# Two projections behind the shared expert's last steps, and list pairs taken five in four experts

## The chip, the core and the metric

The kernel runs on one core of a Trainium2 chip. A core has engines with queues of their own, each in order: TensorE (PE in the profile: matrix products; PEld is its loading of weights), VectorE (DVE), ScalarE (ACT), GpSimd (POOL) and SyncE (SP, which here only issues DMAs). They meet through semaphores. The metric is the time of the device in microseconds (us), from launch to end; lower is better.

## What is computed

The input x is (2, 1024, 256). It is normalized over its last axis (mean and variance, eps 1e-5) to xn. The result is x + attention(xn) + ffn(xn).

The attention reads xn as tokens of 16 numbers on a 64 x 64 grid. One product makes q, k and v. Two branches of 8 channels each attend inside windows of 8 tokens, one along rows, one along columns, with softmax(q k / sqrt(8)) v, and add a 3 x 3 depthwise convolution of v (its window is one token wide, so only three taps of each filter count). A projection, a layernorm with weights and a residual of the tokens follow, and a transpose of tokens and channels.

The ffn is a mixture of 16 experts for 2048 rows of 256, with hidden width 176, and a shared expert of width 352:

```
out[row] = sum over the row's 6 experts e of  weight[row, e] * (silu(x Wg[e]) * (x Wu[e])) Wd[e]
         + (silu(x Sg) * (x Su)) Sd
```

The six experts are chosen by a sigmoid gate with a bias: the two best of four groups of experts, then the six best of what is left. Everything is float32.

## The kernel before

**Stages.** First (to about 60 us) the rows are loaded, normalized and turned (`xnT`), the gate is computed, and each row gets a key by its choice of experts. A sort by that key puts the 2048 rows into 16 tiles of 128, so that rows of a tile share most of their experts. For each tile the six most frequent experts are computed for all its rows, with weight 0 where a row hasn't chosen one: 96 experts in all (kind "six"). What is left over (rows that chose an expert outside their tile's six) is gathered into lists of 128 rows, 14 of them worked off in the main loop (kind "extra") and any rest in a loop at the end.

**The shared expert** is a generator (`shared_steps`, L266) whose steps are taken out by `meanwhile(until)` (L317) between other work: products (L275), the gate on ScalarE (L283) and its product with the other half on VectorE (L284, into `room`), and down products (L290) with the copy and bias on ScalarE (L291). `meanwhile(100)` at L1113 takes all steps that are still left, those of the last block of 512 rows.

**The attention** is a list of steps with costs (`attention`, L657), one head after another: four heads (two halves of the batch, two halves of the columns). A head gathers rows (L670), makes eight projections (`project`, L673: one product on TensorE, L675, and four copies on ScalarE, L677 to L680), four products of q and k (L688) and their sums (L692) on VectorE, the softmax (L698 to L704, with the exponential on ScalarE at L700), four products with v (L709) and sums (L714), the division (L722, `xo`), and transposes on TensorE (L729) with copies on ScalarE (L731, `oT`). The first product of q and k needs projections 0 to 3, the second 4 to 7. After the four heads, `attended` and `normed` project, normalize and add (L781 to L806).

**The main loop** (L1124) runs over 55 units of two experts each (48 "six", 7 "extra"); i = 2u + q counts experts. For each expert, `begun` makes the two up products (L867), the silu on ScalarE (L869, `sg`), and the weighted product on VectorE (L870, `hms`). There are three PSUM buffers for the up products, so an expert can't start before the VectorE step of the third one before it is done. A unit's hidden values are turned one unit later (`hidden`, L881), and the down products follow one unit after that (L893, or L901 for an extra). A finished tile is scattered with accumulation to the output by GpSimd (`to_out`, L1008). Tiles of sorted rows are fetched by GpSimd (`asked`, L827) and turned (`sorted_tile`, L835) ahead of use. `walked` (L1096) takes attention steps in between, as many as the planner's costs allow (`done`, `pace`). Ahead of the loop it is called once with a fixed limit of `FIRST_ROWS - LEAD` (L1111), where the counted time starts at -LEAD and each of the head's first steps (the gathering and the eight projections) counts 0.3.

**The lists** come from a generator, `lists_begun` (L914), of which the loop takes one step per expert from i = 14 on (L1134). After three steps of preparation on VectorE come the pairs of expert and tile that are left over, up to NX = 26, one per step: `pair_listed` reads a column with a register from a table on ScalarE (L967, `spot`, two buffers), and makes a one-hot matrix for it with two GpSimd operations (L969, L970, four buffers in `ysum`). A product on TensorE (L960, `rows_of`) adds it to the lists, two pairs behind. At the end `lists_ended` (L973) turns the sums into row numbers on VectorE (L976, L977), and the extras' rows are gathered by them on GpSimd (`gathered`, L994), one unit ahead of use. The first extra is the 49th expert, i = 48.

**The order.** The source's order is not the queues' order: a scheduler, working from its own estimates while the program is built, places each instruction in its engine's queue. So a small change of the source can move many instructions.

Of the kernel before, what the change touches and what calls it, by code (L numbers as in the profile page):

```python
# [22 lines left out]
P = 128  # L23
# [20 lines left out]
NX = 26  # L44
# [7 lines left out]
def csw_block_moe(ctx: ExitStack, tc: tile.TileContext, x, qkv_w, conv_w0, conv_b0, conv_w1, conv_b1,  # L52
# [20 lines left out]
    nc = tc.nc  # L73
# [78 lines left out]
    for c in range(16):  # L152
        n = sum(P // 2 if k % 2 == 0 else P for k in range(c)) + (((16 - c) * P - 1) / 2 if c % 2 == 0 else 0)
# [380 lines left out]
    for c in range(15, -1, -1):  # L534
        n = 16 - c
# [8 lines left out]
        for k in range(1, n):  # L544
            nc.tensor.matmul(down_[:, c + k : c + k + 1], lhsT=beats[:, k, :], rhs=less[:, c % 2 : c % 2 + 1], start=False,
                             stop=(c == 0 and k == 15))
# [25 lines left out]
    for n in range(2):  # L572
        nc.vector.tensor_tensor(ohp[:, 8 * n : 8 * n + 8], row_h.unsqueeze(1).to_broadcast(wide),
                                place[:, 1, 8 * n : 8 * n + 8].unsqueeze(2).to_broadcast(wide), ALU.is_equal)
        for c in range(8 * n, 8 * n + 8):
# [38 lines left out]
                     start=True, stop=True)  # L614
# [297 lines left out]
    listed = []  # L912

    def lists_begun():  # L914
        flagged = room_[:, 832:960].bitcast(BF16)
        behind = room_[:, 960:1024].bitcast(BF16)
        spot = room_[:, 1024:1280]
        spoti = [t.bitcast(I32) for t in (room_[:, 1280:1536], ysum[:, 7])]
        by_pair = flagged.rearrange("p (e t) -> p e t", t=NTL)
        nc.vector.scalar_tensor_tensor(by_pair, wsrt.rearrange("p t e -> p e t"), 0.0, kept, op0=ALU.is_gt, op1=ALU.mult)  # L920
        nc.vector.tensor_scalar(behind, row_h, part_no, None, op0=ALU.is_gt)
        before = ps_m.tile([P, 2, E * NTL], F32, tag="m", name="before")
        nc.tensor.matmul(before[:, 0], lhsT=behind, rhs=flagged, start=True, stop=True)
        nc.tensor.matmul(before[:, 1], lhsT=ones, rhs=flagged, start=True, stop=True)
        yield
        rows_, some, upto = small.tile([P, E], F32, name="rows_"), small.tile([P, E], I32, name="some"), begin[:, 1]
        nc.vector.tensor_reduce(out=rows_, in_=before[:, 1].rearrange("p (e t) -> p e t", t=NTL), axis=AX.X, op=ALU.add)
        nc.vector.tensor_scalar(some, rows_, P - 1.0, None, op0=ALU.add)
        nc.vector.tensor_scalar(some, some, 7, None, op0=ALU.logical_shift_right)
        nc.vector.tensor_copy(begin[:, 0], some)  # L930
        one_e = one_f.to_broadcast([P, E])
        nc.vector.tensor_tensor_scan(ends, one_e, begin[:, 0], 0.0, op0=ALU.mult, op1=ALU.add)
        nc.vector.tensor_tensor(begin[:, 0], ends, begin[:, 0], ALU.subtract)
        nc.vector.tensor_tensor_scan(upto, one_e, rows_, 0.0, op0=ALU.mult, op1=ALU.add)
        nc.vector.tensor_tensor(upto, upto, rows_, ALU.subtract)
        nc.vector.scalar_tensor_tensor(begin[:, 0], begin[:, 0], float(P), upto, op0=ALU.mult, op1=ALU.subtract)
        nc.vector.tensor_tensor_scan(spot, one_f.to_broadcast([P, E * NTL]), before[:, 1], 0.0, op0=ALU.mult, op1=ALU.add)
        nc.vector.tensor_tensor(spot, spot, before[:, 1], ALU.subtract)
        nc.vector.tensor_tensor(spot, spot, before[:, 0], ALU.add)
        wide = [P, E, NTL]  # L940
        nc.vector.tensor_tensor(spot.rearrange("p (e t) -> p e t", t=NTL), spot.rearrange("p (e t) -> p e t", t=NTL),
                                begin[:, 0].unsqueeze(2).to_broadcast(wide), ALU.add)
        yield
        nc.vector.tensor_copy(spoti[0], spot)
        nc.vector.tensor_scalar(spoti[1], spoti[0], 7, None, op0=ALU.logical_shift_right)
        nc.vector.tensor_scalar(spoti[0], spoti[0], P - 1, None, op0=ALU.bitwise_and)
        nc.gpsimd.memset(at_[:, :, 0:1], 0.0)
        for n in range(2):
            nc.scalar.copy(at_[:, n, 1:], spoti[n])
        nc.vector.tensor_tensor(at_[:, 2, 1:].rearrange("p (e t) -> p e t", t=NTL), by_pair,  # L950
                                of_f.unsqueeze(1).to_broadcast(wide), ALU.mult)
        listed.append(ps_t.tile([P, NX], F32, tag="y1", name="rows_of", padded_shape=[P, TB]))
        yield
        spots = {}
        for n in range(NX + 2):
            if n < NX:
                spots[n] = pair_listed(n)
            if n >= 2:
                spot = spots.pop(n - 2)
                nc.tensor.matmul(listed[0], lhsT=spot[:, 0:P], rhs=spot[:, P:], start=(n == 2), stop=(n == NX + 1))  # L960
            yield
        lists_ended()
        yield

    def pair_listed(n):
        spot = small.tile([P, 3], F32, name="spot", tag="spot")
        nc.scalar.copy(spot, at_[:, :, bass.ds(number(xrow[0:1, 0, n : n + 1], ACT, NTL * E), 1)].rearrange("p a n -> p (a n)"))  # L967
        spots = room_[:, 1024 + 80 * (n % 4) :][:, 0 : (P + NX) // 2].bitcast(F16)
        nc.gpsimd.tensor_scalar(spots[:, 0:P], row_h, spot[:, 0:1], None, op0=ALU.is_equal)  # L969
        nc.gpsimd.tensor_scalar(spots[:, P:], row_h[:, 0:NX], spot[:, 1:2], spot[:, 2:3], op0=ALU.is_equal, op1=ALU.mult)  # L970
        return spots

    def lists_ended():  # L973

        none = room_[:, 1500 : 1500 + NX]
        nc.vector.tensor_scalar(none, listed[0], 0.0, ROWS + 1.0, op0=ALU.is_equal, op1=ALU.mult)  # L976
        nc.vector.scalar_tensor_tensor(lists[:, 0:NX], listed[0], -1.0, none, op0=ALU.add, op1=ALU.add)  # L977

        over = room_[0:1, 0 : NX * E].rearrange("p (n e) -> p n e", e=E)
        of_list = room_[0:1, 500 : 500 + NX]  # L980
        nc.vector.tensor_tensor(over, ends[0:1].unsqueeze(1).to_broadcast([1, NX, E]),
                                number_f[0:1, 0:NX].unsqueeze(2).to_broadcast([1, NX, E]), ALU.is_le)
        nc.vector.tensor_reduce(out=of_list, in_=over, axis=AX.X, op=ALU.add)
        nc.vector.tensor_scalar(xrow[:, 2, 0:NX], of_list, E - 1.0, None, op0=ALU.min)
        nc.vector.tensor_copy(xrow[:, 1, 0:NX], number_f[0:1, 0:NX])

        some = small.tile([1, 2], F32, name="some_")
        nc.vector.scalar_tensor_tensor(some[:, 0:1], pairs_[0:1], NX + 0.5, pairs_[0:1], op0=ALU.is_gt, op1=ALU.mult)
        nc.vector.tensor_tensor(some[:, 0:1], some[:, 0:1], ends[0:1, E - 1 : E], ALU.max)
        nc.vector.tensor_scalar(left, some[:, 0:1], -float(NL), 0.0, op0=ALU.add, op1=ALU.max)  # L990
# [93 lines left out]
    of_tile = (0.75, 0.25)  # L1084
    END = 84
    in_walk = [4 * (16 * 2.3 + 3.3 + 2.5 + 1.5 + 1.4) + 0.6 + 8 * 1.4, 4 * 6.2 + 8 * 3.9]
    FIRST_ROWS, LEAD = 2.5, 12
    done = [float(-LEAD), 0.0]
    whole = [in_walk[n] + NTL * TOPK * of_slot["six"][n] + NL * of_slot["extra"][n] + NTL * of_tile[n] for n in range(2)]
    pace = (whole[0] - LEAD - END * of_slot["six"][0] / of_slot["six"][1]) / (whole[1] - END)  # L1090
# [1 line left out]
    def counted(cost):  # L1092
        for n in range(2):
            done[n] += cost[n]
# [22 lines left out]
    begun_, hT_ = {}, {}  # L1117
    waiting = []
    extras_, lists_ = extras_listed(), lists_begun()

    def fetched(u):
        middle(wts[:, u % 3], *(expert_of(laid_out[u], q, SP) for q in range(2)))

    for u in range(len(laid_out) + 2):  # L1124
        for q in range(2):
            i = 2 * u + q

            while tiles_sorted < NTL and 5 * (tiles_sorted - 2) <= 6 * (i - 2):
                sorted_tile(tiles_sorted)
                counted(of_tile)  # L1130
                tiles_sorted += 1
            while len(asked_for) < min(NTL, tiles_sorted + 3):
                asked()
            if i in (2, 4, 8) or i >= 14:  # L1134
                next(extras_ if i < 14 else lists_, None)
            if u + 1 < len(laid_out) and laid_out[u + 1][0] == "extra":
                n = laid_out[u + 1][1] + q
                ahead[n] = gathered(lists[:, n : n + 1])
            if u < len(laid_out):
                if q == 0:  # L1140
                    fetched(u)
                begun_.setdefault(u, []).append(begun(laid_out[u], q, hms[:, u % 2]))
            if q == 1:
                if 0 <= u - 1 < len(laid_out):
                    hT_[u - 1] = hidden(hms[:, (u - 1) % 2])
                if 0 <= u - 2 < len(laid_out):
                    finished(laid_out[u - 2], hT_.pop(u - 2), wts[:, (u - 2) % 3], begun_.pop(u - 2))
            counted(of_slot[laid_out[min(u, len(laid_out) - 1)][0]])
            walked()
            if done_:  # L1150
                to_out(*done_.pop(0))
            while waiting:
                waiting.pop(0)()
# [73 lines left out]
```

## Time and profile before

| | us |
|---|---|
| median of 3 runs | 449.53 (446.91 to 451.74) |
| the profiled execution | 448.94 |
| its span | 447.2 |
| TensorE busy | 393.4 |
| VectorE busy | 293.0 |
| ScalarE busy | 215.6 |
| GpSimd busy | 187.8 |
| mean granted clock of TensorE | 0.978 |

In the lines that follow, a row of the timeline gives the start from the span's start, the duration, the engine, the line of the kernel, the operation, what it writes and reads, and in square brackets the idle time before it and what ended that. A row of the waits gives the engine and what it was about to do, for whom it waited, the total, the number of times and the longest. A row of the windows gives the length, then busy time and count for PE, PEld, DVE, ACT and POOL, then the granted clock of TensorE (1.00 is full speed), the DMA engines' share and GB/s. Starts of successive VectorE instructions can lie closer than their durations, so sums of times are made from starts.

### The profile page before, as it was taken

The numbers are of one execution on the slowest core, as the hardware profiler recorded it, in microseconds if no ns is written. First come the engines' busy times: TensorE is split into PE (matmuls) and PEld (weight loads), VectorE is DVE, ScalarE is ACT, GpSimd is POOL, SyncE is SP. The second block draws the span as 40 slices with busy tenths as digits, with TensorE's granted clock in tenths as the row PEclk, the third lists the DMA queues.
The fourth block names the chain that finished last, engine by engine and source line by source line (L and its number), as shares of the span: only waits on it lengthen the run. The fifth ranks groups of instructions, "written<-read, shape, count | busy, mean of one in ns | idle before, by whom it ended". The sixth has DMA issues, their size and how long they took to land. (4 is left out here: it accounts for less than half of the span.)

```text
span 447.2 us, 6291 instructions
## 1 busy us (share of the span) xinstructions
PE 393.4 (88%) x1668; PEld 247.4 (55%) x1669; DVE 293.0 (66%) x515; ACT 215.6 (48%) x535; POOL 187.8 (42%) x207
## 2 busy tenths in 40 slices
PE   0999999997887979898898899999899999999970
PEld 0445565655554646665565476566655555666750
DVE  4627958679997948979779599398992333322110
ACT  2955247462472355372462452735335777843220
POOL 7400000220556145886504235324542778791431
PEclk9999999998999999999999699999999999999995
DMA  8999942320423110121012133202331129347222
GB/s 236 314 290 328 272 170 42 48 82 12 86 70 85 22 20 22 33 38 39 22 24 45 52 60 65 44 20 63 85 58 38 22 65 141 74 70 101 44 33 24
DMA packets 40178, 37.56 MB, mean 84 GB/s; under 512 B 5300, under 2 KB 37616, under 8 KB 40112
## 3 DMA queue, kind: packets, MB, share of 16 engines
q0 software_dynamic: 11616, 13.52, 18.4%
q1 hardware_dynamic: 27472, 22.59, 16.6%
q10 hardware_dynamic: 1056, 1.05, 0.7%
q8 instruction: 15, 0.25, 0.2%
q14 instruction: 19, 0.16, 0.1%
HBM read 27.70 MB, written 12.45 MB: 90 GB/s over the span
## 5 line engine op out<-in xcount | busy, mean ns | idle before, releaser
L867 PE MATMUL pr_u<-w1s,xsT 128*128 x384 | 128.3, 468 | 2.7 <-DVE hms L870 2.1
L867 PEld LDWEIGHTS pr_u<-w1s,xsT 128*128 128x128 f32 x384 | 69.9, 190 | 39.3 <-issue 7.1
L1008 POOL DMA_INDIRECT out_dram<-ysum,lists x30 | 51.0, 1701 | 88.5 <-ACT ysum L1047 38.0
L869 ACT ACTIVATE sg<-pr_u 128x176 f32<-128x176 f32 x110 | 34.6, 317 | 83.1 <-PE pr_u L867 73.6
L870 DVE SCALAR_TENSOR_TENSOR hms<-sg,w,pr_u 128x176 f32<-128x176 f32 x96 | 37.4, 392 | 49.1 <-ACT sg L869 46.6
L688 DVE TENSOR_TENSOR pr<-qk 128x2048 f32<-128x2048 f32 x16 | 36.6, 2288 | 15.8 <-ACT qk L677 15.3
L709 DVE TENSOR_TENSOR pv<-s,v 128x2048 f32<-128x2048 f32 x16 | 36.6, 2286 | 4.2 <-ACT s L700 4.2
L692 DVE TENSOR_REDUCE s<-pr 128x256 f32<-128x2048 f32 x16 | 36.5, 2281 | 0.1
L714 DVE TENSOR_REDUCE o<-pv 128x256 f32<-128x2048 f32 x16 | 36.4, 2272 | 0.0
L293 POOL DMA_DIRECT2D out_dram<-ysum x4 | 3.7, 914 | 76.1 <-ACT ysum L291 76.1
L881 PEld LDWEIGHTS ph<-ident,hms 128*128 128x128 f32 x165 | 21.4, 141 | 19.8 <-issue 8.0
L994 POOL DMA_INDIRECT xg<-xw_d,lists x14 | 21.2, 1512 | 26.2 <-DVE hms L870 23.7
L881 PE MATMUL ph<-ident,hms 128*128 128x128 f32 x165 | 29.5, 276 | 2.2 <-DVE hms L870 1.7
L969 POOL TENSOR_SCALAR ysum<-row_h,spot 128x128 f16<-128x128 f16 x26 | 21.3, 825 | 23.4 <-PE rows_of L960 17.0
L827 POOL DMA_INDIRECT xg<-xw_d,lists x16 | 21.6, 1353 | 18.7 <-PE px__1007 L835 6.5
L893 PE MATMUL pr_y<-w2a,hT 128*128 x96 | 28.7, 380 | 0.0
L893 PE MATMUL pr_y<-w2b,hT 112*128 x96 | 28.7, 379 | 0.0
L893 PE MATMUL pr_y<-wts,hT 128*128 128x256 f32 x96 | 28.5, 379 | 0.0
L290 PE MATMUL py<-room 128*128 128x256 f32 x96 | 25.3, 402 | 2.5 <-DVE room L284 2.5
L883 ACT COPY hT<-ph 128x384 f32<-128x384 f32 x55 | 26.3, 479 | 1.9 <-PE ph L881 1.2
L675 PE MATMUL pq<-wq,rows 128*128 128x384 f32 x64 | 24.8, 503 | 2.5 <-ACT oT L731 1.4
L867 PE MATMUL pr_u<-w1s,xd 128*128 x56 | 21.8, 518 | 5.1 <-ACT xd L1003 4.6
(403 smaller groups left out, 703.6 us busy)
## 6 DMA issues: line engine op xcount, KB each, us to landing
w1s<-in_w_dram SPq DMA_DIRECT2D x22, 256.0 KB
wts<-in_w_dram SPq DMA_DIRECT2D x55, 64.0 KB
wts<-in_w_dram SPq DMA_DIRECT2D x55, 48.0 KB
xw_d<-xx SPq DMA_DIRECT2D x4, 544.0 KB
w2a<-in_w_dram SPq DMA_DIRECT2D x4, 512.0 KB
out_dram<-ysum POOLq DMA_DIRECT2D x4, 512.0 KB, 6.8
xr<-xw_d POOLq DMA_DIRECT2D x4, 512.0 KB
out_dram<-att POOLq DMA_DIRECT2D x8, 256.0 KB, 4.1
```

The lines of the kernel that those rows point to most:

```text
L290: nc.tensor.matmul(py, lhsT=hms[k, m][:, P * c : P * c + P], rhs=w2h[:, m], start=(m == 0), stop=(m == 2))
L688: nc.vector.tensor_tensor(pr, q_.unsqueeze(3).to_broadcast(full), k_.unsqueeze(2).to_broadcast(full), ALU.mult)
L692: nc.vector.tensor_reduce(out=s[:, n : n + NW], in_=held.pop(n), axis=AX.X, op=ALU.add)
L709: nc.vector.tensor_tensor(pr, s[:, n : n + NW].unsqueeze(3).to_broadcast(full), v[:, br, m : m + NW].unsqueeze(2).to_broadcast(full), ALU. ...
L714: nc.vector.tensor_reduce(out=o[:, n : n + NW], in_=held.pop(n), axis=AX.X, op=ALU.add)
L867: nc.tensor.matmul(pu, lhsT=lhs[:, h, :], rhs=w1s[:, :, h, bass.ds(e * I, I)], start=(h == 0), stop=(h == 1))
L869: nc.scalar.activation(sg, pu[:, 0, :], AF.Silu)
L870: nc.vector.scalar_tensor_tensor(hm[:, 0:I], sg, w, pu[:, 1, :], op0=ALU.mult, op1=ALU.mult)
L881: nc.tensor.transpose(ph[:, s, :], units[:, P * s : P * s + P], ident)
L883: nc.scalar.copy(hT, ph)
L893: nc.tensor.matmul(py, lhsT=l_, rhs=r_, start=start and n == 0, stop=stop and n == 2)
L1008: nc.gpsimd.indirect_dma_start(out=out_rows, out_offset=bass.IndirectOffsetOnAxis(ap=index, axis=0), in_=ys, in_offset=None, bounds_check= ...
```

## The change

Three constants and one call:

```
-        for n in range(NX + 2):
+        for n in range(NX + 3):
             if n < NX:
                 spots[n] = pair_listed(n)
-            if n >= 2:
-                spot = spots.pop(n - 2)
-                nc.tensor.matmul(listed[0], lhsT=spot[:, 0:P], rhs=spot[:, P:], start=(n == 2), stop=(n == NX + 1))
+            if n >= 3:
+                spot = spots.pop(n - 3)
+                nc.tensor.matmul(listed[0], lhsT=spot[:, 0:P], rhs=spot[:, P:], start=(n == 3), stop=(n == NX + 2))
             yield
...
-    FIRST_ROWS, LEAD = 2.5, 12
+    FIRST_ROWS, LEAD = 2.0, 12
...
             if i in (2, 4, 8) or i >= 14:
                 next(extras_ if i < 14 else lists_, None)
+            if i > 16 and i % 4 == 0:
+                next(lists_, None)
```

With `FIRST_ROWS` at 2.5 the call at L1111 takes the gathering and all eight projections of the first head; with 2.0 it takes six, and the last two come with the next call at L1114, behind `meanwhile(100)`. The second call of `next(lists_)` takes a further step at i = 20, 24, 28 and so on, so five steps in four experts, and `lists_ended` comes at i = 40 in place of 45. The product that adds a pair comes three pairs behind its making in place of two. The number of instructions of each engine stays the same. In the built order, SyncE's queue is unchanged, and those of the other engines differ in the stretch between the sixth projection and the first extras; VectorE, ScalarE and GpSimd also have some neighbours swapped in the head behind that.

## Prediction

> **What bounds the kernel now.** I read the page's slices first, then the windows, the waits and, at each long gap, the timeline. The profiled execution took 448.94 us, 1.74 around its span of 447.2; the three runs have a median of 449.53, so 0.6 is added to what follows from the trace.
>
> ```profile
> PE 393.4 (88%) x1668; PEld 247.4 (55%) x1669; DVE 293.0 (66%) x515; ACT 215.6 (48%) x535; POOL 187.8 (42%) x207
> ```
>
> TensorE is the busiest engine, but it isn't alone in setting the end. The windows show where it stands still: 40.00 us hold 35.08 of TensorE at 240 to 280, and 39.52 at 360 to 400. From 95 to 315 VectorE works through four heads of attention with hardly a pause, and TensorE's fixed order makes it wait for that. After the last head (337) come the attention's epilogues, then eight scatters, each waiting for the one before to land:
>
> ```profile
> 435.08 1.54 POOL L1008 DMA_INDIRECT out_dram<-ysum,lists  x1 [1.91 <-DMA out_dram<-ysum,lists]
> 439.61 1.54 POOL L1008 DMA_INDIRECT out_dram<-ysum,lists  x1 [2.99 <-DMA out_dram<-ysum,lists]
> ```
>
> So what counts is how early TensorE and VectorE get through the last head. A gain on TensorE after 400 would be worth nothing; one before 337 moves everything behind it.
>
> In the built orders of both kernels, TensorE's instructions differ from the sixth projection (98 us) to the expert numbered 40 (221 us, counting from 0), apart from where the last `rows_of` stand. From there both run the same list. Two long gaps of TensorE lie inside or just behind this stretch:
>
> ```profile
> 106.07 1.29 PE L290 MATMUL py<-room 128*128 128x256 f32 x4 [2.52 <-DVE room L284]
> 247.04 0.69 PE L1001 MATMUL px__2528<-ident,xg 128*128 128x128 f32 x2 [3.09 <-DMA xg<-xw_d,lists]
> ```
>
> The first waits for VectorE's gate product of the shared expert, which stands behind a second attention product. The second is the first listed group, whose rows are fetched late because the lists are late:
>
> ```profile
> 241.85 0.18 DVE L977 SCALAR_TENSOR_TENSOR lists<-rows_of,ysum 128x26 int32<-128x26 f32 x1
> 242.50 2.64 POOL L994 DMA_INDIRECT xg<-xw_d,lists  x1 [0.30 <-issue]
> ```
>
> Both gaps are followed by a slow clock. In the answer by windows (busy and count of each engine, then PEclk), the third line is a like stretch without a gap:
>
> ```profile
> 107.00:113.30 6.30, 6.30 (x21) 4.68 (x21) 6.09 (x5) 2.02 (x5) 0.41 (x1) 0.74 0.01 3
> 247.00:255.80 8.80, 7.74 (x21) 4.63 (x22) 3.88 (x5) 4.40 (x6) 1.61 (x2) 0.62 0.18 47
> 268.20:274.10 5.90, 5.09 (x23) 3.52 (x22) 5.90 (x5) 1.65 (x5) 2.56 (x2) 1.00 0.35 54
> ```
>
> **Part 1: lists five in four.** From 243.95 to 255.80 TensorE does the work of two listed groups, one set of turned rows and one down product: 11.85 us. The next such set takes 5.90 (third line above). If the rows are there in time, 5.95 us go: 3.09 and 0.64 of waiting, 2.2 of slow clock. In the new order the last `rows_of` stands before expert 40, and VectorE makes the lists just behind the second head's output (before, 23 us behind it, at 241.85). From the lists to the landing took 5.0 us (242.03 to 247.04). With lists at some 226, rows land by 232; TensorE wants them at 244 to 250. The cover is 12 us or more, so I count all of -5.95. What is late next is nothing at that place.
>
> The order holds two calls in a row at every fourth expert. A call brings one copy on ScalarE (0.19), two operations on GpSimd (0.60 and 0.46, one pair each 1.03), one product on TensorE (0.18). Their number stays 26; nothing is added to the sum of work, and the DMA queue of SyncE has the same order. What changes is who waits. GpSimd needs 5 x 1.03 = 5.2 us per four experts, beside 10.0 (expert 24 at 180.5, expert 28 at 190.5). It isn't the bound by this: it waited 17.0 for TensorE. But each operation that meets VectorE's product of two tensors stops until that ends:
>
> ```profile
> 172.86 2.56 POOL L970 TENSOR_SCALAR ysum<-row_h,spot 128x26 f16<-128x26 f16 x1
> ```
>
> This one takes 0.46 without a neighbour. The waits tell who pays (us in total, times, longest):
>
> ```profile
> ACT spot L967 <- POOL ysum L970: 23.1, 17, 4.0
> POOL ysum L969 <- PE rows_of L960: 17.0, 7, 5.3
> ```
>
> ScalarE stands at `spot` until GpSimd is done, and behind it in its queue are the gates (`sg`), for which VectorE and then TensorE wait.
>
> **Part 2: two projections later.** `room L284` now stands ahead of the second product, so it ends at 103.8 and not at 106.0. TensorE's gap shrinks from 2.52 to about 2.0 (101.9 to 103.9), as it has less to do in between. But projections six and seven follow two down products each. From 103.9: 1.3 for the rest of the first two down sets, 0.75 for the projection, 1.4 and 1.4 for the other two sets, 0.75 for the last projection: 109.5, and its copy on ScalarE stands behind two bias copies. VectorE's second product needs it and starts at 110.1, before at 103.13. VectorE idles from 104.0, that is 6.1 us. Queued behind it are all gate products, so experts wait too: TensorE's first late gates are some 1.2 us at expert 5's turn, 3.7 at expert 11. Yet expert 11 starts at 138.9, in the old trace at 139.1 (there TensorE waited for rows), so this is no loss on TensorE.
>
> VectorE's first head took 61.75 us, 98.42 to 160.17, with 2.9 idle (0.59, 1.05, 1.01 and small ones). These vanish when it is late, so the head ends at 98.4 + 58.9 + 6.1 = 163.4, 3.2 later. TensorE has cover: expert 20 and two smaller steps, 3.7 us of work, now stand ahead of the transposes of the head's output.
>
> Then comes the handover to the second head: transposes, copies, projections, first product.
>
> ```profile
> 168.08 2.29 DVE L688 TENSOR_TENSOR pr<-qk 128x2048 f32<-128x2048 f32 x1 [3.70 <-ACT qk L677]
> ```
>
> It took 168.08 - 160.17 = 7.9. In the new order three `rows_of` follow the transposes at once, where there was one, and ScalarE has six more `spot` copies ahead of the first projection's. Pairs 0 to 2 are ready at 165.3, 166.3 and 167.7, so TensorE stands 2.5 us (before 1.28 and 0.73 here); the copies reach the first projection at 171.1 (pairs each 1.03 from 164.2), and the product starts at about 174.1: 10.7 us, 2.8 more.
>
> The second head took 50.65 (168.08 to 218.75) with 3.8 idle. From 174.1 this makes 224.8, when before it was 218.75. TensorE used to get there at 221.1, 2.3 us later, and must now wait: +4.1 at the transposes. Bounds: if the handover isn't lengthened and VectorE idles only for the exponential (2.0), 220.2, TensorE isn't held, +0.5 from the remaining gaps; if gates are held behind GpSimd, another 4 us, +8. I take +4.1, since the idle of 3.8 is the trace's own.
>
> [...]
>
> **Sum.** -5.95 + 4.1 + 0.7 = -1.2. On its own time 447.8, on the median 448.4. I say 448.
>
> **Rivals.** *The handover costs nothing* (clearly faster). The copies ahead of the projections find GpSimd unhindered, since VectorE is idle then and no product stops it; then only 0.5 is lost and -5.4 stays: 444. For it speaks that TensorE, not VectorE, was late by 2.3 at the second handover. Against it the six copies in ScalarE's order.
>
> *ScalarE held by GpSimd* (slower). From 180 to 220, a spot copy can't go until the pair two before is done. With pairs closer, one more collision with a product costs 2.56 - 0.46 = 2.1. Per four experts GpSimd needs 5.2, about 1.3 for scatters, and 2.1 for each collision: two make 10.7 against 10.0 us. From the third on it decides: 12.8, so 2.8 per round, over four rounds 11 us at the handover in place of 4.1: 448.4 + 7 = 455. Against it: three pairs in flight where two were, and 17.0 us of slack.
>
> *The lists aren't earlier in effect*: they stand behind the second head's output on VectorE. They'd gain nothing only if that came after 239, 14 us past my estimate; then 454. Small, put with the slower.
>
> **How the numbers follow.** A measurement here tells about 1% from no change. My forecast 0.57 (446 to 451 by its own terms), the fast handover 0.25, slower cases 0.18. The range from 443.5 (-5.4 on the median) to 453.5 (a delay of 8 and another cold stretch) leaves out some 0.2.
>
> **What would show it.** Right: no wait for rows at the first listed group and full clock at 245 to 260; VectorE idle some 6 us at 104 to 110; the second head's first product at 172 to 176; its output near 225, with TensorE waiting for it. Wrong: that product at 170 or before (then faster), or ScalarE's wait for `ysum L970` well above 23.1 and gates late from 180 on (then slower).

## The result and the profile after

The changed kernel takes 451.42 us (median; 449.93 to 453.46) where the kernel before takes 447.65 (446.27 to 451.74): the ratio is 1.0072, with a 95% interval of 1.0055 to 1.0089. So it is some 3.2 us slower. The forecast was 448.0, 1.5 below the 449.53 known then: the time moved the other way.

The profiled execution took 452.02, its span 450.3. First the page's row of busy times:

```profile
PE 391.7 (87%) x1668; PEld 246.2 (55%) x1669; DVE 291.8 (65%) x515; ACT 215.4 (48%) x535; POOL 186.7 (41%) x207
```

No engine has more work than before; what was lost is lost in waits. The timeline of TensorE shows the gaps:

```profile
102.04 1.13 PE L290 MATMUL py<-room 128*128 128x256 f32 x4 [1.85 <-DVE room L284]
...
140.74 0.41 PE L835 MATMUL px__1371<-ident,xg 128*128 128x128 f32 x2 [4.33 <-DMA xg<-xw_d,lists]
...
206.28 2.61 PE L867 MATMUL pr_u<-w1s,xsT 128*128 x4 [2.53 <-DVE hms L870]
...
227.32 1.09 PE L729 MATMUL po<-ident,xo 128*128 128x128 f32 x8 [0.98 <-DVE xo L722]
...
249.78 0.38 PE L1001 MATMUL px__2528<-ident,xg 128*128 128x128 f32 x2
```

The two gaps that the change was expected to shrink did so: 2.52 became 1.85 at L290, and 3.09 at the first listed group became nothing. New are 4.33 at the 13th tile's rows, where before had 1.72, and 2.53 in the second head. The windows, in the columns of before, show the listed set at full clock. Over the stretches with the two new gaps the mean clock is 0.85 and 0.76, with 3.41 us at 0.50 in each (from 141.56 and from 206.41):

```profile
249.70:255.55 5.85, 5.05 (x24) 3.39 (x23) 5.85 (x7) 2.26 (x6) 0.69 (x1) 1.00 0.10 24
136.40:148.00 11.60, 7.27 (x29) 5.22 (x29) 8.68 (x17) 2.93 (x8) 5.28 (x4) 0.85 0.27 70
203.70:210.90 7.20, 4.67 (x16) 3.10 (x15) 7.20 (x7) 4.40 (x14) 3.27 (x6) 0.76 0.03 10
```

VectorE's timeline holds the rest of the forecast's landmarks: the late second product, a wait for the same rows, the first product of head 2 behind a gate that came late, and the lists.

```profile
107.38 2.29 DVE L688 TENSOR_TENSOR pr<-qk 128x2048 f32<-128x2048 f32 x1 [5.31 <-ACT qk L677]
...
145.48 0.18 DVE L838 COPY wsrt<-xg 128x16 f32<-128x16 f32 x1 [2.50 <-DMA xg<-xw_d,lists]
...
171.89 0.40 DVE L870 SCALAR_TENSOR_TENSOR hms<-sg,w,pr_u 128x176 f32<-128x176 f32 x1 [7.24 <-ACT sg L869]
172.99 2.29 DVE L688 TENSOR_TENSOR pr<-qk 128x2048 f32<-128x2048 f32 x1 [0.71 <-ACT qk L677]
...
227.78 0.17 DVE L977 SCALAR_TENSOR_TENSOR lists<-rows_of,ysum 128x26 int32<-128x26 f32 x1
```

In the two traces VectorE's first product of head 1 starts 1.6 us apart (98.42 before, 96.79 after), and the change acts from about there on, so I count from it and call this the landmarks' clock. The landmarks, in us from there, are rows of L688 and L722 in the timelines (the last two rows are the parts of the change by themselves, from the first two experiments below):

| | last output of head 1 | first product of head 2 | last output of head 2 | first product of head 3 | first product of head 4 |
|---|---|---|---|---|---|
| before | 61.08 | 69.66 | 119.64 | 128.41 | 189.69 |
| after | +4.37 | +6.54 | +10.15 | +7.93 | +3.06 |
| projections late alone | +4.76 | +6.93 | +7.53 | +5.31 | +6.39 |
| lists five in four alone | +0.40 | +0.40 | +1.95 | +1.95 | -3.28 |

The last column stands close to the measured times (3.2 slower, 7 slower, 3.9 faster), so the whole story lies between the first and the fourth head. The lists give back what they were meant to, between the last two columns. The projections take more, at three places: in head 1, at the handover to head 2 (from head 1's last output to head 2's first product), and, for the most part only together with the lists, in head 2.

### The profile page after: what moved, and what is told of

Same layout as the page of the kernel before. It is cut to its first block, busy times and chain, and to the rows that moved or that the text cites. A ratio compares the mean times of both kernels' runs of the same rounds, so it can differ in the third digit from the quotient of the medians.

```text
span 450.3 us, 6289 instructions
## 1 busy us (share of the span) xinstructions
PE 391.7 (87%) x1668; PEld 246.2 (55%) x1669; DVE 291.8 (65%) x515; ACT 215.4 (48%) x535; POOL 186.7 (41%) x207
## 5 line engine op out<-in xcount | busy, mean ns | idle before, releaser
L867 PE MATMUL pr_u<-w1s,xsT 128*128 x384 | 130.1, 473 | 5.1 <-DVE hms L870 4.4
L867 PEld LDWEIGHTS pr_u<-w1s,xsT 128*128 128x128 f32 x384 | 71.1, 193 | 42.0 <-issue 8.0
L1008 POOL DMA_INDIRECT out_dram<-ysum,lists x30 | 52.1, 1735 | 93.9 <-ACT ysum L1047 35.8
L870 DVE SCALAR_TENSOR_TENSOR hms<-sg,w,pr_u 128x176 f32<-128x176 f32 x96 | 37.3, 394 | 52.9 <-ACT sg L869 52.9
L688 DVE TENSOR_TENSOR pr<-qk 128x2048 f32<-128x2048 f32 x16 | 36.6, 2289 | 17.5 <-ACT qk L677 17.1
L709 DVE TENSOR_TENSOR pv<-s,v 128x2048 f32<-128x2048 f32 x16 | 36.6, 2286 | 4.7 <-ACT s L700 4.7
L969 POOL TENSOR_SCALAR ysum<-row_h,spot 128x128 f16<-128x128 f16 x26 | 27.4, 1072 | 24.9 <-ACT spot L967 11.9
L881 PE MATMUL ph<-ident,hms 128*128 128x128 f32 x165 | 31.4, 280 | 5.8 <-DVE hms L870 5.1
L994 POOL DMA_INDIRECT xg<-xw_d,lists x14 | 20.7, 1478 | 24.3 <-DVE hms L870 21.0
L827 POOL DMA_INDIRECT xg<-xw_d,lists x16 | 20.9, 1309 | 22.3 <-DVE hms L870 8.1
L290 PE MATMUL py<-room 128*128 128x256 f32 x96 | 24.1, 388 | 1.9 <-DVE room L284 1.9
L867 PE MATMUL pr_u<-w1s,xd 128*128 x56 | 19.9, 481 | 5.6 <-ACT xd L1003 5.6
```

Source lines behind the costliest of these rows:

```text
L688: nc.vector.tensor_tensor(pr, q_.unsqueeze(3).to_broadcast(full), k_.unsqueeze(2).to_broadcast(full), ALU.mult)
L709: nc.vector.tensor_tensor(pr, s[:, n : n + NW].unsqueeze(3).to_broadcast(full), v[:, br, m : m + NW].unsqueeze(2).to_broadcast(full), ALU. ...
L867: nc.tensor.matmul(pu, lhsT=lhs[:, h, :], rhs=w1s[:, :, h, bass.ds(e * I, I)], start=(h == 0), stop=(h == 1))
L870: nc.vector.scalar_tensor_tensor(hm[:, 0:I], sg, w, pu[:, 1, :], op0=ALU.mult, op1=ALU.mult)
L881: nc.tensor.transpose(ph[:, s, :], units[:, P * s : P * s + P], ident)
L1008: nc.gpsimd.indirect_dma_start(out=out_rows, out_offset=bass.IndirectOffsetOnAxis(ap=index, axis=0), in_=ys, in_offset=None, bounds_check= ...
```

## The experiments

The kernel before ran anew in each comparison (medians of 448.95 to 449.19, where the result above has 447.65), so kernels of different comparisons are set side by side by their ratios to it. Intervals that overlap leave the difference open.

**Each part alone.** The first theory: the late projections cost more than the forecast's 4.1, and the lists gain nearly all of theirs. The rival: the lists' denser pairs are what costs. Edits: the changed kernel with one of the two parts taken back.

```
 first:   for n in range(NX + 2): ... (two behind), no second next(lists_); FIRST_ROWS = 2.0 stays
 second:  FIRST_ROWS, LEAD = 2.5, 12; the lists' three edits stay
```

> The limit of 2.0 alone; the lists as before (one step per expert, products two pairs behind). In its built order the stretch up to the second head's first product is that of the changed kernel: the 13th fetch of rows on GpSimd stands behind the first scatter, three rows_of follow the transposes, and the copies of the first projection stand behind those of four pairs. Theory A (the two late projections cost, the lists gain): 453 to 456, +6 to +8 on the kernel before; the transposes of the second head come 6 to 8 us later by the trace; the wait for rows at the first listed group stays. Theory B (the closer pairs cost, the projections are free): 447 to 449.

> Five list steps in four experts and products three pairs behind, with the limit left at 2.5. Theory A: 441 to 443, -5 to -6.5, the wait for rows at the first listed group and the half clock behind it gone, and nothing given back. Theory B: 447 to 451, gates late between the first and the second head's end, ScalarE's wait for GpSimd's pairs above 23 us.

Measured: 456.27 with late projections alone, ratio to before 1.0154 (1.0128 to 1.0180), and 445.13 with the lists alone, 0.9913 (0.9897 to 0.9930). So +6.9 and -3.9, whose sum is +3.0 beside the +3.2 of both together. By their times the parts add. The projections are as the first theory has them; the lists gain, but less than their 5.95, and 445.13 lies between the two theories' ranges. With late projections alone the old wait at the first listed group is still there:

```profile
251.82 0.44 PE L1001 MATMUL px__2528<-ident,xg 128*128 128x128 f32 x2 [3.12 <-DMA xg<-xw_d,lists]
```

**Two suspects in the trace of after.** One is ScalarE held by GpSimd: a spot copy waits for the pair two before it, and gates stand behind. The other is the late fetch of the 13th tile. The edits, each on the changed kernel:

```
-        nc.scalar.copy(spot, at_[...])
+        nc.gpsimd.tensor_copy(spot, at_[...])
```
```
-        xg = work.tile([P, ROW], F32, tag="xg", name="xg", bufs=3)
+        xg = work.tile([P, ROW], F32, tag="xg", name="xg", bufs=4)      (sums: bufs=1)
```

> The changed kernel with the column of each pair copied by GpSimd, not by ScalarE: the orders of TensorE and ScalarE are those of the changed kernel, but ScalarE no longer waits for pairs; GpSimd gets 26 more copies. If ScalarE held by GpSimd delays the first projection's copies and the gates: the handover (head's output to next product) falls from 10 to some 8 us, VectorE's idle time in the second head from 7 to 4, and the time to 445 to 447. If the gates are late for other reasons (VectorE's own order, TensorE's): 450 to 452, or later by GpSimd's added copies.

> The changed kernel with four buffers for fetched rows in place of three (and one for the softmax sums, whose writer and reader are both on VectorE). The fetches of the 13th and 14th tile stand ahead of the first scatter. If the late fetch is a cost of its own: the gap of 4.3 us at 136 to 141 and the half clock behind it go, VectorE no longer waits 2.5 for rows at 143, and the time falls by 2.5 to 3.6, to 448 to 449. If VectorE's late chain swallows it: 451, with the gain of TensorE lost again at the transposes of the first or second head.

Measured: 450.15, 1.0019 (0.9997 to 1.0041), and 451.08, 1.0053 (1.0032 to 1.0073). Neither is the whole cause. Without copies on ScalarE the changed kernel's ratio falls by 0.0053, some 2.4 us, but not as expected: in its trace (of an execution of 452.99, 2.8 above the median) the handover takes 11.48 and VectorE's idle time in head 2 is 6.6. The waits of that kernel show that TensorE now waits for the pairs itself (2.0 in total in the changed kernel).

```profile
PE rows_of L960 <- POOL ysum L970: 7.2, 7, 2.1
```

With a fourth row buffer the 4.33 gap is gone and head 1 ends 1.9 earlier than in the changed kernel, but its handover takes 12.06 in place of 10.75, and the time moves by 0.8, which the overlapping intervals don't tell from nothing.

**The handover.** In the changed kernel's ScalarE timeline, spot copies stand ahead of the copies of the first head's transposes and of the first projection's, and most wait for a pair:

```profile
165.56 0.19 ACT L967 COPY spot<-ysum 128x3 f32 x1 [0.83 <-POOL ysum L970]
165.72 1.94 ACT L731 COPY oT<-po 128x512 f32<-128x512 f32 x2
...
168.84 0.19 ACT L967 COPY spot<-ysum 128x3 f32 x1 [1.06 <-POOL ysum L970]
169.86 0.19 ACT L967 COPY spot<-ysum 128x3 f32 x1 [0.83 <-POOL ysum L970]
169.96 0.26 ACT L677 COPY qk<-pq 128x128 f32<-128x128 f32 x1
```

With late projections alone the handover takes 10.76, so it is the late projections, through the scheduler's order, that lengthen it, and not the denser pairs. I began the pairs three experts later and took them four in three; then the same with four row buffers; and, as a dose of the first head's idle, the projections between the shared expert's down products. In the same comparison, the lists alone with four row buffers.

```
-            if i in (2, 4, 8) or i >= 14:
+            if i in (2, 4, 8, 14, 15, 16) or i >= 20:
...
-            if i > 16 and i % 4 == 0:
+            if i > 20 and i % 3 == 0:
```
```
+    meanwhile(spent[0] + 6)
+    walked(2.5 - LEAD)
     meanwhile(100)
     walked()
```

> The changed kernel with its pairs begun at the 21st expert in place of the 18th and taken four in three, so that they still end at the 43rd (before the change the 46th, with the change the 41st). No pair's product is left between the transposes of the first head's output and the second head's projections, and no spot copy stands ahead of the first projection's copies. In the changed kernel ScalarE lost 1.06 and 0.83 there to GpSimd's pairs, and the transposes' own copies came 1.3 late behind two more. If the lengthened handover (10.76 from the last output of head 1 to the first product of head 2, against 8.59 before) is a cause with a price of its own: it shrinks to about 8.2 and the time falls by some 2.5, to 449. If the denser pairs in head 2 hold ScalarE as long as it saves: 451 to 452. If the first half's delay (first output 4.4 late on its own clock) is all that counts: no change, 451.4.

> The same with four buffers for fetched rows in place of three (and one for the softmax sums), so that the 13th tile's rows are not late either. Four row buffers alone brought head 1 forward by 1.9 on VectorE's own clock but lengthened the handover by 1.3 and the time moved by 0.3. If the handover swallowed that gain through the pairs in ScalarE's and TensorE's order, both gains add here: 451.4 - 2.5 - 1.9 = 447. If the handover is bound by something else (the projections, the transposes' copies): no more than 0.5 below the run without the buffers.

> The changed kernel with the last two projections between the shared expert's first two and last two down products, and so neither ahead of all (before) nor behind all but the last (the change). VectorE's second product starts some 1.5 earlier than in the changed kernel (its idle falls from 5.3 to about 3.8). If VectorE's idle is passed on one to one, as rows alone suggests (+7.2 for 5.3 of idle and what follows): about -1.5 to -2, 449.5 to 450. If what counts is the order of GpSimd's fetch and scatter and the handover, which this edit leaves as in the changed kernel: 451 to 452.

> Lists five in four without the late projections (445.1, the fastest so far), with four row buffers. There TensorE lost 1.44, 0.97 and 1.71 waiting for fetched rows of the 6th, 9th and 13th tile, with 3.4 of half clock behind the last. If those waits have a price of their own: -2 to -3, 442 to 443. If VectorE's first head sets the pace there, as with the changed kernel's: within 0.5 of 445.

The pairs behind the handover: 449.19, ratio 1.0001 (0.9981 to 1.0022), 0.0071 or 3.2 us below the changed kernel. The handover takes 8.60, as before the change, and VectorE's wait for a gate in it is 4.96 where it was 7.24. Head 2 is 1.5 shorter too (52.1), as this edit also moves the pairs in it. The trace is of the fastest of 13 executions.

```profile
170.20 0.40 DVE L870 SCALAR_TENSOR_TENSOR hms<-sg,w,pr_u 128x176 f32<-128x176 f32 x1 [4.96 <-ACT sg L869]
```

With four row buffers as well: 449.16, 0.9996 (0.9969 to 1.0023), no further gain. Head 1 does end 2.1 earlier, but the handover takes 11.87. The built order now has six spot copies ahead of the transposes' copies, where it had four, the last of them in ScalarE's timeline being

```profile
166.92 0.19 ACT L967 COPY spot<-ysum 128x3 f32 x1 [0.83 <-POOL ysum L970]
167.09 1.92 ACT L731 COPY oT<-po 128x512 f32<-128x512 f32 x2
```

The chain of pairs starts when the lists' preparation is through on VectorE, 1.2 us behind head 1's last output in both kernels, and runs at one pair per 1.02. So the two copies more take back 2.0 of the 2.1: on the landmarks' clock the transposes' copies start at 69.28 without the row buffers and at 69.19 with them. This is what swallowed the buffers' gain.

The projections between the down products were a miss: 453.61, 1.0108 (1.0068 to 1.0149), no faster than the changed kernel (the intervals overlap), though VectorE's idle fell from 5.31 to 2.72. TensorE's timeline shows that the 13th tile's rows came hardly earlier (43.7 on the landmarks' clock, 43.95 in the changed kernel):

```profile
141.06 0.41 PE L835 MATMUL px__1371<-ident,xg 128*128 128x128 f32 x2 [3.67 <-DMA xg<-xw_d,lists]
```

Head 1's last output comes at 66.15, in the changed kernel at 65.45. That with three row buffers the fetches hold it as much as VectorE does is read from this, not tested apart.

The lists alone with four row buffers: 444.05, 0.9878 (0.9849 to 0.9907), about 1.5 below the lists alone by the ratios, whose intervals overlap. The expected 442 to 443 was too much.

**The pace, and the projections with the other suspects taken away.** First the pace alone, with the products two pairs behind. Then three kernels with four row buffers and the lists begun later, that differ in the projections' place: behind (as changed), early (as before), between.

```
-            if i in (2, 4, 8) or i >= 14:
+            if i in (2, 4, 8) or i >= 18:
...
-            if i > 16 and i % 4 == 0:
+            if i > 21 and i % 2 == 0:
```

> Of the three parts of the change, the pace alone: five pairs in four experts, but with the products two pairs behind and the projections where they were. With lists five in four and the products three behind 445.1 was measured. If the third pair of distance is what lets the denser pairs pass (TensorE's product waits for GpSimd when only two are between): 447 to 448, little or no gain over before (448 to 449). If the distance costs and saves nothing and the pace does it all: 445 within 1.

> The changed kernel with both other suspects taken away: four row buffers (the 13th tile's rows not late), and the lists' preparation begun at the 19th expert in place of the 15th, the pairs at the 22nd, three in two, so that in the built order no spot copy stands ahead of the copies of the first head's transposes. The two projections still come behind the shared expert's last steps. To be compared with the two that follow, which differ from it in the projections' place alone (in the source). If VectorE's idle of 5.3 at the start of the first head is passed on: 4 to 5 above the one with the projections where they were, some 448. If the late rows and the pairs were the whole cost: within 1.5 of it, some 444 to 445.

> The same buffers and the same late lists, with the projections where they were before the change. Expected 443 to 444 (lists five in four with four row buffers gave 444.05, and its handover of 8.6 may shrink by 0.5 to 1 more without spot copies ahead of the transposes' copies); 446 if pairs three in two, as dense as they must be for this late start, hold the gates in head 2.

> The same once more, with the two projections between the shared expert's first two and last two down products: VectorE's idle 2.7 in place of 5.3 and 0. With the rows' fetch late, this dose did nothing (453.6, where the changed kernel has 451.4). If VectorE's idle is passed on when nothing else is late: half way between the two before, some 446. If it isn't: like both.

The pace alone: 446.21, 0.9930 (0.9904 to 0.9956). The interval overlaps that of the lists with the third pair of distance, 0.9913: the pace does it, and the distance can't be told from nothing.

The three others: late 448.27, 0.9975 (0.9947 to 1.0004); early 447.81, 0.9965 (0.9940 to 0.9990); between 441.88, 0.9829 (0.9787 to 0.9872). Head 1 ends at 60.62, 55.17 and 56.31: with the fetches out of the way VectorE's idle is passed on to the end of its head, 5.45 of it when late, 1.1 when between. But the times don't follow. On VectorE's clock the early one still has 3.9 of its 5.45 at head 2's first product. TensorE lost more at this handover, where its timeline has

```profile
167.89 2.93 PE L675 MATMUL pq<-wq,rows 128*128 128x384 f32 x4 [4.07 <-ACT v L680]
```

as the scheduler had put six spot copies ahead of the fifth projection's copies; in the kernel with the projections between none stands ahead of these. TensorE then comes to head 2's transposes 5.4 us behind VectorE's last output, in the late kernel 0.7. The windows of the handover, here of the early kernel and below of the one with the projections between:

```profile
159.70:174.00 14.30, 10.10 (x25) 5.88 (x24) 7.18 (x4) 6.32 (x36) 6.16 (x8) 0.76 0.01 2
```
```profile
157.80:172.20 14.40, 14.15 (x52) 8.56 (x52) 10.33 (x14) 9.50 (x48) 6.59 (x10) 1.00 0.06 17
```

In 14.3 us the one has TensorE busy for 10.1, at 0.76 of the clock, and the other for 14.15 at 1.00: 25 products against 52. But the first trace is of the slowest of 12 executions (451.64) and the second of the fastest of 6 (440.07), so the traces differ by twice what the medians do. The second is the fastest kernel of the study, by 1.7% against the kernel before.

**The projections' price once more.** The lists begun one expert later still, so that in the built order no spot copy stands in the handover at all (the lines replaced are left out here).

```
+            if i in (2, 4, 8) or i >= 19:
...
+            if i > 22 and i % 2 == 0 or i > 34:
```

> As the kernel with late projections uncovered, but the lists' preparation begins one expert later (the 20th), and the pairs at the 24th, so that in the built order no spot copy stands between the second head's projection copies at all. Four row buffers. If VectorE's delay in the first head (5.4 in the traces of the uncovered kernels) is the price of the late projections and passed on to the end: 4 to 6 above the next kernel, some 445. If TensorE's second handover absorbs part of it, as when the projections were late alone (6.9 at the second head's start, 5.3 at the third's): 3 to 4 above.

> The same with the projections where they were before the change. The uncovered kernel with early projections had its second projection group wait 4.07 for ScalarE's copies behind spot copies, and 447.8. If those copies were what ate the 5.4 that its first head had gained: 440 to 442. If it was something else, such as TensorE being the bound from there on: 446 to 448 again.

> The same with the projections between the shared expert's down products (441.9 with the lists begun one expert earlier, where no spot copy stood ahead of its second projection group either). If that time came from the clean handover: 441 to 443 again, and within 1.5 of the kernel with early projections, as the first head's ends differed by 1.1. If the place of the projections gave it: 4 or more below the kernel with early projections.

Late 452.63, 1.0110 (1.0074 to 1.0146); early 450.18, 1.0027 (0.9999 to 1.0055); between 450.63, 1.0042 (1.0021 to 1.0062). Late projections cost 2.5 by the medians and 3.7 by the ratios, near the expected 3 to 4; between costs nothing that can be told. But all three are 8 to 10 slower than a clean handover was expected to make them. The handovers are clean, head 2 starts at 63.0 to 65.2 (before 69.66) and then takes 63.3 to 64.7 us to its last output, where it took 50.0. The pairs now fall within some 18 experts, where they had 28 before the change. In the early kernel VectorE's idle makes 9.9 of the 14.3 more (13.7 against 3.8); its longest wait is for a gate behind six spot copies in a row, and the pairs hold TensorE itself:

```profile
186.46 0.40 DVE L870 SCALAR_TENSOR_TENSOR hms<-sg,w,pr_u 128x176 f32<-128x176 f32 x1 [4.89 <-ACT sg L869]
```
```profile
181.95 0.18 PE L960 MATMUL rows_of<-ysum 128*128 128x26 f16 x1 [2.69 <-POOL ysum L970]
```

The rest of the 14.3 is work: only in these three kernels does the lists' preparation fall into head 2 (4.5 us of VectorE instructions), and one or two more experts' gate products with it. So pairs cost where spot copies in a row stand ahead of a gate. How many fall into head 2 doesn't tell by itself: 22 with the lists alone (51.5 us) and with the pairs behind the handover (52.1), 19 in the changed kernel (53.6). What is left open: in the three kernels before these, pairs come three in two as well, yet head 2 took 53.7 in the one with the projections between and 59.4 and 59.5 in the two others, with 7.2, 12.3 and 12.7 of VectorE idle. The built orders differ in many places there, and no run separates them.

## Why the prediction was wrong

**What held.** The lists: the forecast counted -5.95 at the first listed group, and the trace has -6.6 there (TensorE's up products of the 51st expert, right behind the first listed set, start at 158.76 on the landmarks' clock, 1.37 later than before, when head 3 had begun 7.93 later). The gap at L284 (about 2.0 forecast, 1.85). VectorE's idle (6.1 forecast, 5.31). The 2.3 us by which TensorE had been late at the transposes were absorbed as forecast (+10.15 at head 2's last output, +7.93 at head 3's first product). The first product of head 2 (174.1 forecast on the clock of before; 76.20 behind 98.42 is 174.6) is in part luck: head 1 ended 1.2 later than forecast, and the handover grew by 2.2 in place of 2.8 (the forecast counts it from the head's end, the table from the start of its last output). The forecast has six more spot copies ahead of the first projection's; in the trace eight stand there, and five before the change. And the lower end of its range, 443.5, is -5.4 from the profiled execution, not from the median, where it makes 444.1.

**What failed first: "expert 11 starts at 138.9, in the old trace at 139.1 ..., so this is no loss on TensorE".** The step took the rows' arrival from the old trace. But GpSimd's order had changed: the 13th fetch stands behind the first scatter, and that waits for a copy. Before:

```profile
133.20 3.41 POOL L827 DMA_INDIRECT xg<-xw_d,lists  x1 [0.30 <-PE ph L881]
136.92 1.65 POOL L1008 DMA_INDIRECT out_dram<-ysum,lists  x1 [0.30 <-issue]
```

After:

```profile
133.71 1.65 POOL L1008 DMA_INDIRECT out_dram<-ysum,lists  x1 [3.09 <-ACT xsT L836]
135.66 3.15 POOL L827 DMA_INDIRECT xg<-xw_d,lists  x1 [0.30 <-DVE hms L870]
```

On the landmarks' clock the fetch is issued at 38.87 in place of 34.78. So TensorE stood for 4.33 and VectorE for 2.50 more, and head 1's inner idle, which the forecast let vanish, stayed (8.2 us of idle in head 1 against 2.9): head 1 ended 4.4 later, not 3.2. Taking the late rows away gained little (0.8 with row buffers alone, nothing on top of the moved pairs), since the handover's chain of pairs swallowed it.

**What failed most: "The second head took 50.65 with 3.8 idle ... I take +4.1, since the idle of 3.8 is the trace's own".** On the landmarks' rows the head took 53.6 from first product to last output (before 50.0), its idle was 7.2 (1.39, 0.29, 1.61, 0.80, 2.34, 0.80; before 3.8), and TensorE reached the transposes 7.85 later, not 4.1. The forecast's own upper bound (+8, "if gates are held behind GpSimd") was what happened. Its reason for the lower value, that the old trace's idle stays, left out what the second call does to ScalarE's order: it puts a second spot copy ahead of a gate.

Neither part makes this alone: head 2 takes 50.6 with late projections alone and 51.5 with the lists alone. The first of these runs has the same collision at the same place as the changed kernel, an `L970` of 2.89 us (after, at 184.86) beside the third product of q and k. There a gate stands ahead of the spot copy that waits for it (ScalarE's timeline, late projections alone):

```profile
186.39 0.31 ACT L869 ACTIVATE sg<-pr_u 128x176 f32<-128x176 f32 x1
189.24 0.19 ACT L967 COPY spot<-ysum 128x3 f32 x1 [2.54 <-POOL ysum L970]
```

In the changed kernel two spot copies follow each other and the gate stands behind them, so VectorE waits for it:

```profile
184.83 0.19 ACT L967 COPY spot<-ysum 128x3 f32 x1 [0.22 <-POOL ysum L970]
187.78 0.19 ACT L967 COPY spot<-ysum 128x3 f32 x1 [2.76 <-POOL ysum L970]
188.14 0.32 ACT L869 ACTIVATE sg<-pr_u 128x176 f32<-128x176 f32 x1 [0.16 <-issue]
```
```profile
188.49 0.40 DVE L870 SCALAR_TENSOR_TENSOR hms<-sg,w,pr_u 128x176 f32<-128x176 f32 x1 [1.61 <-ACT sg L869]
```

Ahead of the head's first product with v, VectorE waits 0.80 and 2.34, where the run with late projections alone has 1.31: a gate and the exponential stand behind a spot copy that waited 3.35 for GpSimd, which had a scatter (1.60) and two stretched pair operations (1.92 and 1.45) to do. TensorE's gap of 2.53, shown above, comes behind that. These waits make 3.4 more and one of 0.50 is gone, about the 3.0 between 50.6 and 53.6. No edit puts that one spot copy back behind its gate, so this is read from two traces and not tested. With the spot copies on GpSimd no gate stands behind one, and head 2 still took 52.9, as TensorE waited for the pairs there.

More or longer collisions are not the difference. The mean of L969 rose from 825 ns to 1072, but the collision above is there with late projections alone too, where head 2 took 50.6: the denser pairs set who waits behind it.

The slower rival had this wait and this place, but it counted added collisions; its price of 7 was too high beside the 3.6 us by which head 2 grew. The sign by which it was to be known, ScalarE's total wait, hardly moved:

```profile
ACT spot L967 <- POOL ysum L970: 25.4, 19, 4.3
```

25.4 against 23.1: the total doesn't tell (with late projections alone it is 27.0, and head 2 took 50.6); who stands behind each wait does.

**What was left out.** The lists alone gained 3.9 and not 5.95, for two reasons that the table shows: denser pairs lengthen head 2 by 1.5 even when nothing is late (1.6 with the pace alone), and of the 6.6 that TensorE gains by the first listed group, 1.3 are given back in head 3 (1.7 in the changed kernel). Head 3 took VectorE 51.75 to its last output before, with the wait for the listed rows in it, and 47.51 after; it shrank by less than TensorE gained.

**The sum as it came out:** +7.93 at head 3's start, -6.56 at the first listed set, +1.69 in head 3: +3.06. The forecast had +4.1, -5.95 and +0.7 for the clock. The mis-sized term is head 2 with the transposes behind it, by 3.8: 7.9 where the forecast took 4.1.

**The clock.** No run shows the +0.7 that the sum has for the clock; it was the author's estimate. In its place the traces have 10.24 us at half clock between 30 and 430 before (3.41 from 106.92 and 6.83 from 246.86) and 6.82 after (3.41 from 141.56 and from 206.41). The shrunken gap of 1.85 at L290 was not followed by half clock (1.00 from 102.02 to 105.43), the new ones of 4.33 and 2.53 were, and so was one of 2.42 at L290 with the lists alone (0.50 from 104.40 to 107.80).

## What to carry to other kernels

When a change reorders work under a scheduler, follow every queue that the built order changes, GpSimd's fetches and scatters too: a row's arrival read from the old trace holds only if its issue keeps its neighbours. Helper work that passes through three engines (here ScalarE, GpSimd, TensorE: 0.19, 1.03 and 0.18 us a pair) costs little by its busy time and much by what stands behind its waits; look where its chain runs beside the critical handovers, and whether two of its steps in a row stand ahead of something that the busy engines wait for. Gains of separate repairs don't add when one chain, here the pairs, catches up with each of them: place that chain first.

## What the hardware showed that I had not expected

Between 30 and 430 us half clock (0.50) came in stretches of 3.41 us (before, from 106.92; after, from 141.56 and 206.41) or twice that (before, 6.83 from 246.86), and the length of the gap ahead didn't decide. Gaps of 1.72 (before, at 138.55), 1.85 (after, at 102.04) and 2.27 (late projections alone, at 103.11) weren't followed by one, while 1.71 with the lists alone was:

```profile
137.15 0.41 PE L835 MATMUL px__1371<-ident,xg 128*128 128x128 f32 x2 [1.71 <-DMA xg<-xw_d,lists]
```

How little TensorE had worked just ahead doesn't tell by itself either. In the 3.41 us ahead of the four slow stretches of before and after it was busy for 0.89, 0.50, 0.82 and 0.88. With the lists alone it was busy for 1.55 and half clock followed; from 98.60 to 102.02 after, with the gap of 1.85 in it, it was busy for 1.58 of 3.42 and the next 3.41 us ran at 1.00. What decided was not shown. The 3.41 us ahead of the slow stretch and the slow stretch, with the lists alone:

```profile
135.14:138.55 3.41, 1.55 (x7) 0.84 (x6) 3.30 (x5) 0.69 (x2) 2.70 (x3) 1.00 0.41 69
138.55:141.95 3.40, 3.40 (x11) 2.46 (x10) 1.19 (x5) 0.80 (x2) 1.91 (x2) 0.50 0.48 114
```

Two windows that hold the gap of 2.27, with late projections alone:

```profile
98.55:101.97 3.42, 2.29 (x10) 1.49 (x8) 3.39 (x2) 0.11 (x1) 2.42 (x1) 1.00 0.10 19
101.97:105.38 3.41, 2.27 (x10) 1.83 (x11) 1.17 (x3) 1.36 (x6) 0.00 (x0) 1.00 0.06 22
```

And the issue of a fetch on GpSimd, 0.95 beside a reduction on VectorE (after, at 139.11), took 3.15 and 3.41 (the two rows of the 13th fetch above) beside a product of two tensors (L709, 2.27, from 135.65 after and from 133.49 before). Of the pairs' operations, not "each operation that meets VectorE's product of two tensors" was held: of the eight L969 and L970 of before that overlap a 128x2048 product, five took 0.67 to 3.01 us, and three, begun 0.23 to 0.51 ahead of it, took 0.45 to 0.60. A fetch's issue begun 0.05 ahead of a product (after, at 127.46) took 0.96.
